# Graph network with mixture-of-experts layers: masks, scaling, weight loads and message buffers in the sum by source rearranged

## The chip, the cores and the metric

The kernel runs on one core of a Trainium2 chip. A core has five engines, each with a queue of its own that it works off in order: TensorE (PE; its weight loads are listed apart as PEld), VectorE (DVE), ScalarE (ACT), GpSimd (POOL) and SyncE (SP), which here only issues transfers. Sixteen DMA engines move data between device memory and the on-chip memory, SBUF; TensorE writes its products to PSUM, from which VectorE or ScalarE take them. The metric is the device time of one execution in microseconds, the median of several.

## The reference

Node features `x` (6250 x 256, float32) pass four residual blocks: a graph convolution with a two-layer perceptron, a top-2 mixture of 8 experts, a relational graph convolution with 8 relations, and a top-2 mixture of 6 experts. There are 100,000 edges, sorted by their `dst` and in random order of `src`. The change is in the first block and in the dispatch of its result to the experts of the second:

```python
norm = dinv[row_sl] * ew_sl * dinv[col_sl]      # row = src, col = dst, with self loops
msgs = xw[col_sl] * norm[:, None]               # one message for each edge
h7 = segment_sum(msgs, row_sl, num_segments=N) + b
h = relu(h7 @ W1 + b1); out = h @ W2 + b2
...
logits = tokens @ router_w.T                    # top-2 experts for each node
h = gelu(tokens @ w1[e] + b1[e]); y = h @ w2[e] + b2[e]
```

So each node sums the messages of the edges of which it is the source, the sum is scaled by `dinv` of that node, goes through the perceptron, and is then routed to two experts.

## The kernel before

Nodes are cut into 49 blocks of 128, which lie in SBUF as `acc` (the sums) and `X` (the features). The program runs in stages: it builds tables of the edges; it makes the messages and writes each to a place in device memory that puts the edges of one source block together (`msgs`, L858, by indirect transfers from GpSimd); it sums the messages by source and sends each finished block of nodes to the experts (`sum_and_send`, L1181); it runs the experts' tiles (L1297 to L1357); then come the relational convolution and the last experts.

The change lies in the sum stage. `sum_messages` (L874) works through 830 tiles of 128 messages in chunks of 8, so 104 chunks. For one chunk SyncE loads `g` (128 x 8 x 260 floats, 1040 KB, L880); VectorE computes `key` (L882), the place of each message's node within its block, or a value that fits none; eight one-hot masks `m` (128 x 128) are then made by comparing the row of lane numbers with the key: VectorE makes four in one instruction (L884) and GpSimd four in four instructions (L892). TensorE multiplies each mask with the tile's messages (L895) into PSUM, of which the pool `p_mm` has four buffers, and VectorE adds the product to the block's place in `acc` (L897). That place is only known at run time, so the address comes from a register, and the framework orders each such addition against every other use of `acc`.

The pool `sum` gives `g` and `key` three buffers each (`bufs=3`, L1185), and `m` two. A load of a chunk waits until TensorE has done the last tile of the chunk whose buffer it takes.

`send_group` (L1063) takes four finished blocks at a time. It is written as a generator: after each tile of the sum (L1198 to L1200) one piece of it is put in, so that its work is mixed with the sums. For each block it scales the sum by `dinv` (`h7`, L1072, on ScalarE), transposes it on TensorE, applies bias and Relu on ScalarE (L466), multiplies by `W2` (L1089), normalizes, computes the router's logits (L1110, L1119), picks two experts with some fifty small VectorE instructions, and writes each node's row to its two experts' places with eight indirect transfers from GpSimd (L1170). The group of blocks is started when a fixed number of tiles is summed (L1200).

The order of the instructions on each engine is fixed when the program is built: a scheduler of the framework takes the instructions as they are written, with its own estimates of their lengths, and places them in each engine's queue. An instruction that waits holds all that stand behind it on its engine.

Ahead of the stage, SyncE loads the first weights of the eight experts (`fw1`, eight transfers of 256 KB, L1027 through L1010) and their biases as rows (`fb1`, 1 MB written, L1028 through L1020); the second weights and biases (L1212, L1213) follow the stage. `sum_and_send` is built twice, for graphs whose blocks are done late and early (L1207 to L1210); the early one (tags with an `e`, as `pa0e`) runs here.

Of the kernel before, what the change touches and what calls it, by code (L numbers as in the profile page):

```python
# [8 lines left out]
F32 = mybir.dt.float32  # L9
# [5 lines left out]
AF = mybir.ActivationFunctionType  # L15
OP = mybir.AluOpType
# [4 lines left out]
D = 256  # L21
# [21 lines left out]
RW = 260  # L43
# [13 lines left out]
def gnn_ffn_kernel(ctx: ExitStack, tc: tile.TileContext, a, out):  # L57
    nc = tc.nc

    const = ctx.enter_context(tc.tile_pool(name="const", bufs=1))  # L60
# [5 lines left out]
    def psum_mm(name):  # L66
        return p_mm.tile([128, 512], F32, tag="mm", name=name)
# [36 lines left out]
    ones = const.tile([128, 128], F32, name="ones")  # L104
    nc.vector.memset(ones, 1.0)
    lanes_i = const.tile([128, 128], I32, name="lanes_i")
    nc.gpsimd.iota(lanes_i, pattern=[[1, 128]], base=0, channel_multiplier=0)
    lanes = const.tile([128, 128], F32, name="lanes")
    nc.vector.tensor_copy(lanes, lanes_i)
    lanes_h = const.tile([128, 128], BF16, name="lanes_h")  # L110
    nc.vector.tensor_copy(lanes_h, lanes_i)
    rev_i = const.tile([128, 1, 8], I32, name="rev_i")
# [13 lines left out]
    col0, n = {}, 0  # L126
    for name in (
# [8 lines left out]
        k = math.prod(ap.shape) // 128  # L136
# [174 lines left out]
    for q0 in range(0, QN, 4):  # L311
        n = min(4, QN - q0)
# [23 lines left out]
    far = sp.tile([128, QN], F32, name="far")  # L336
# [13 lines left out]
    turn = gap.tile([128, Q * 128], F32, name="turn")  # L350
# [52 lines left out]
    def blocks_of(blk, t0, engines, top):  # L403
        _, v = nc.values_load_multi_w_load_instructions(
            blk[0:1, t0 : t0 + 8],
            engines=engines,
            min_val=0,
            max_val=top,
            skip_runtime_bounds_check_because="it is counted or bounded",
        )  # L410
        return v

    def rsqrt(name, v, shape, pool=None):

        r = work.tile(shape, F32, name=f"{name}_r", tag="rs_r", bufs=1)
        h = work.tile(shape, F32, name=f"{name}_h", tag="rs_h", bufs=1)
        o = (pool or const).tile(shape, F32, name=f"{name}_o", tag="rs_o" if pool else f"{name}_o")
        nc.scalar.activation(h, v, AF.Sqrt)
        nc.vector.reciprocal(r, h)
        nc.vector.tensor_mul(h, r, r)  # L420
        nc.vector.tensor_mul(h, h, v)
        nc.vector.tensor_scalar(h, h, -0.5, 1.5, op0=OP.mult, op1=OP.add)
        nc.vector.tensor_mul(o, r, h)
        return o
# [32 lines left out]
    def transpose_to(name, dest, x, bias=None):  # L457

        pt = p_tr.tile([128, 2, 128], F32, tag="tr", name=f"pt_{name}")
        for k in range(2):  # L460
            nc.tensor.transpose(pt[:, k, :], x[:, k * 128 : (k + 1) * 128], ident)  # L461
        if bias is None:
            nc.scalar.copy(dest, pt)
        else:
            for k in range(2):
                nc.scalar.activation(dest[:, k, :], pt[:, k, :], AF.Relu, bias=bias[k])  # L466
# [224 lines left out]
    firsts = g0p.tile([128, TL], F32, name="firsts")  # L691
# [61 lines left out]
    dinv = rsqrt("deg", deg, [128, NT])  # L753
# [6 lines left out]
    acc = big.tile([128, (NT + 1) * D], F32, tag="big", name="acc0")  # L760
# [113 lines left out]
    def sum_messages(pool, tag):  # L874

        for t0 in range(0, TL, 8):
            n = min(8, T - t0)
            blocks = blocks_of(blks, t0, [ENG.DVE], NT)
            g = pool.tile([128, 8, RW], F32, name=f"g0{tag}_{t0}", tag="g")
            nc.sync.dma_start(g, by_tile[:, t0 : t0 + 8, :])  # L880
            key = pool.tile([128, 8], F32, name=f"key{tag}{t0}", tag="key")
            nc.vector.tensor_sub(key[:, :n], g[:, :n, D], firsts[:, t0 : t0 + n])  # L882
            m = pool.tile([128, 8, 128], F32, name=f"m0{tag}_{t0}", tag="m", bufs=2)
            nc.vector.tensor_tensor(  # L884
                m[:, :4],
                lanes[:, None, :].to_broadcast([128, 4, 128]),
                key[:, :4, None].to_broadcast([128, 4, 128]),
                OP.is_equal,
            )
            for j in range(n):  # L890
                if j >= 4:
                    nc.gpsimd.tensor_scalar(m[:, j], lanes, key[:, j : j + 1], None, op0=OP.is_equal)  # L892
            for j in range(n):
                ps = psum_mm(f"pa0{tag}_{t0 + j}")
                nc.tensor.matmul(ps[:, :D], m[:, j, :], g[:, j, :D], start=True, stop=True)  # L895
                here = acc[:, bass.ds(blocks[j] * D, D)]
                nc.vector.tensor_add(here, here, ps[:, :D])  # L897
                yield t0 + j + 1
# [107 lines left out]
    def load_experts(pool, name):  # L1006
        n_e = a[name].shape[0]
        w = pool.tile([128, n_e, 2, D], F32, name=f"w_{name}")
        for e in range(n_e):
            nc.sync.dma_start(w[:, e], a[name][e].rearrange("(k p) f -> p k f", p=128))  # L1010
        return w


    def rows_of(name, pool):

        v = a[name]
        k = math.prod(v.shape)
        r = pool.tile([128, k], F32, name=f"rows_{name}")
        flat = v.rearrange("(o n) -> o n", o=1) if len(v.shape) == 1 else v.rearrange("e (o n) -> o (e n)", o=1)
        nc.sync.dma_start(r, flat.to_broadcast([128, k]))  # L1020
        return r
# [2 lines left out]
    ys = dram.tile([TE * 128, D], F32, name="ys")  # L1024
    ffn0 = ctx.enter_context(ExitStack())
    fp = ffn0.enter_context(tc.tile_pool(name="ffn0", bufs=1, side="right"))
    fw1 = load_experts(fp, "L0_ffn_w1").rearrange("p e k f -> p (e k f)")  # L1027
    fb1 = rows_of("L0_ffn_b1", fp)  # L1028
    share1 = const.tile([128, NT], F32, name="share1")
    share2 = const.tile([128, NT], F32, name="share2")  # L1030
    ats = const.tile([128, 2, NT], I32, name="ats")
# [31 lines left out]
    def send_group(g, n, mlp, tag, seen):  # L1063
# [5 lines left out]
        for i in range(n + 1):  # L1069
            if i < n:  # L1070
                h7 = work.tile([128, D], F32, name=f"h7{tag}_{g + i}", tag="xn", bufs=3)
                nc.scalar.activation(  # L1072
                    h7, acc[:, (g + i) * D : (g + i + 1) * D], AF.Copy, scale=dinv[:, g + i : g + i + 1]
                )
                rows.append(h7)
            if i:
                transpose_to(
                    f"h7{tag}_{g + i - 1}",
                    uT[:, :, (i - 1) * 128 : i * 128],
                    rows[i - 1],  # L1080
                    [b_mlp[:, k : k + 1] for k in range(2)],
                )
            yield
# [97 lines left out]
    def sum_and_send(tag, early):  # L1181


        with (
            tc.tile_pool(name=f"sum{tag}", bufs=3, side="right") as sump,  # L1185
            tc.tile_pool(name=f"mlp{tag}", bufs=1) as mlp,
        ):
            seen, steps, waiting = [], None, list(GROUPS)

            def step(through):  # L1190
                nonlocal steps
                if steps is None and waiting and through(sum(waiting[0])):
                    g, n = waiting.pop(0)
                    steps = send_group(g, n, mlp, tag, seen)
                if steps is not None and next(steps, steps) is steps:
                    steps = None

            for turn in sum_messages(sump, tag):  # L1198
                if early:
                    step(lambda blocks: S_TURNS * blocks + S_SLACK <= turn)  # L1200
            while steps is not None or waiting:
                step(lambda blocks: True)
# [4 lines left out]
    with tc.If(nlate_sv > 0) as late_s_cmp:  # L1207
        sum_and_send("l", False)
    with late_s_cmp.Else():
        sum_and_send("e", True)  # L1210
    fp2 = ffn0.enter_context(tc.tile_pool(name="ffn0b", bufs=1, side="right"))
    fw2 = load_experts(fp2, "L0_ffn_w2").rearrange("p e k f -> p (e k f)")  # L1212
    fb2 = rows_of("L0_ffn_b2", fp2)  # L1213

    def in_stages(stages, items):

        held = [None] * len(stages)
        for i in range(len(items) + len(stages) - 1):
            for k in reversed(range(len(stages))):
                if 0 <= i - k < len(items):  # L1220
                    held[k] = stages[k](*(held[k - 1] if k else items[i]))
# [144 lines left out]
    acc = big.tile([128, (NT + 1) * D], F32, tag="big", name="acc1")  # L1366
# [285 lines left out]
```

## Time and profile before

| | |
|---|---|
| median of 3 runs | 4226.73 us (4225.7 to 4229.28) |
| profiled execution | 4228.4 us, its span 4226.6 us |
| mean granted TensorE clock | 0.92 of full speed |
| busy over the span | PE 3488.2 us, DVE 2093.3, ACT 1194.2, POOL 2266.0 |
| messages made and written (391 to about 1427 us) | GpSimd busy with 782 indirect transfers |
| sum by source and sends (1440 to 2184 us) | 830 tiles, 49 scalings, 98 sends |
| experts' tiles (2209 to 2480 us) | 105 tiles |
| table of the second convolution (2480 to 2955 us) | |
| second convolution and last experts (2955 us to the end) | |

The span is counted from the first instruction to the last. In the profile an instruction is named by its line, its engine, and the tiles it writes and reads (`acc<-acc,pa0e`); an `x` and a number give how many such instructions are in the row. In a timeline, the bracket behind a row is the time that the engine stood idle before it and what ended that wait. Where several waits end together, the profile names the one that came last. SPq is SyncE's queue.

### The profile page before, as it was taken

Reading aid. Unit: us, or ns where it says so; the run is one execution under the profiler, and the core shown is the slowest. Engines: PE = TensorE matmul, PEld = TensorE weight load, DVE = VectorE, ACT = ScalarE, POOL = GpSimd, SP = SyncE. Lnnn points to the kernel's source line nnn. Section 1 sums busy time; section 2 is a strip of 40 time slices with the busy share of each in tenths; the row PEclk is TensorE's granted clock in tenths of the full one; section 3 lists DMA queues with packets and bytes.
Section 4 is the critical chain, followed back from the end, with each engine's and each line's share of the span. In section 5 each row is a group of like instructions: output and inputs, shape, how many; then the busy total and the mean of one; then the engine's idle time right before and its main releaser. Section 6 shows DMA issues by size and latency. Waiting matters only on the chain.

```text
span 4226.6 us, 52427 instructions
## 1 busy us (share of the span) xinstructions
PE 3488.2 (83%) x14645; PEld 2318.7 (55%) x14645; DVE 2093.3 (50%) x5670; ACT 1194.2 (28%) x2567; POOL 2266.0 (54%) x2440
## 2 busy tenths in 40 slices
PE   2887777777777467888869977999579999999999
PEld 1565665565656344555547743444256666666656
DVE  6686211111111146777763358665456666666552
ACT  3312333333333101111114433665012222222213
POOL 1001777777777524555551048333767777777650
PEclk7998999999999778999989988999689999999999
DMA  5514333333333424555543335444645555555540
GB/s 176 168 37 154 129 128 128 128 128 128 127 128 129 148 97 166 182 183 191 182 160 124 109 104 201 196 196 204 191 142 151 150 153 152 150 150 153 143 116 9
DMA packets 233062, 612.03 MB, mean 145 GB/s; under 512 B 41909, under 2 KB 126104, under 8 KB 212784
## 3 DMA queue, kind: packets, MB, share of 16 engines
q0 software_dynamic: 100624, 294.88, 22.3%
q1 hardware_dynamic: 112636, 290.21, 20.4%
q10 hardware_dynamic: 19488, 23.31, 1.5%
q8 instruction: 131, 2.15, 0.2%
q14 instruction: 183, 1.49, 0.1%
HBM read 371.49 MB, written 236.79 MB: 144 GB/s over the span
## 4 chain that ended last, share of the span: by engine, by line
PE 38%; DVE 9%; issue 4%; DMA 2%; ACT 2%; POOL 2%; DVEq 0%; ACTq 0%; POOLq 0%; SPq 0%
PE ph_e1a L473 6%; PE py1a L1001 5%; PE pa1a L922 5%; PE ph_e2a L473 5%; PE phx L1415 4%; PE pf L1334 2%; PE pf L1350 2%; PE pa0e L895 2%; DVE rest L1425 1%; DVE acc L897 1%; DVE acc L926 1%; PE pt_fh L461 1%; DMA g1a<-hx,idxT 1%; DVE hx L1409 1%; PE pcb1a L1517 1%
## 5 line engine op out<-in xcount | busy, mean ns | idle before, releaser
L858 POOL DMA_INDIRECT msgs<-msgn,at x782 | 785.9, 1005 | 550.7 <-DMA rowsn<-lane_rows 312.9
L914 POOL DMA_INDIRECT g1a<-hx,idxT x830 | 828.3, 998 | 323.2 <-PE pa1a L922 144.9
L840 PE MATMUL pxn<-acc,sTn 128*128 x3128 | 790.8, 413 | 243.1 <-DVE sTn L821 216.2
L840 PEld LDWEIGHTS pxn<-acc,sTn 128*128 128x128 f32 x3128 | 613.5, 206 | 420.3 <-DVE sTn L821 282.4
L895 PE MATMUL pa0e<-g0e,m0e 128*128 128x256 f32 x1660 | 502.1, 440 | 186.2 <-DVE acc L897 79.2
L855 ACT ACTIVATE msgn<-pxn,ewT 128x256 f32<-128x256 f32 x782 | 370.0, 473 | 638.4 <-PE pxn L840 451.0
L926 DVE TENSOR_TENSOR acc<-acc,pa1a 128x256 f32 x830 | 346.9, 418 | 343.2 <-PE pa1a L922 312.4
L895 PEld LDWEIGHTS pa0e<-g0e,m0e 128*128 128x128 f32 x1660 | 298.2, 209 | 355.9 <-DVE acc L897 136.2
L892 POOL TENSOR_SCALAR m0e<-lanes,keye 128x128 f32<-128x128 f32 x414 | 265.9, 657 | 346.9 <-PE pa0e L895 274.7
L831 DVE COPY msgn<-srcT 128x32 f32<-128x32 f32 x98 | 18.0, 186 | 830.2 <-DMA msgs<-msgn,at 748.1
L922 PE MATMUL pa1a<-g1a,m1a 128*128 128x256 bf16 x2490 | 374.8, 282 | 54.4 <-DMA g1a<-hx,idxT 38.6
L897 DVE TENSOR_TENSOR acc<-acc,pa0e 128x256 f32 x830 | 347.4, 419 | 126.9 <-ACT h7e L1072 41.6
L922 PEld LDWEIGHTS <-m1a 128*128 128x128 bf16 x2490 | 243.4, 100 | 278.3 <-issue 193.7
L1415 PE MATMUL phx<-wr,xT 128*128 128x512 f32 x784 | 373.5, 621 | 24.9 <-DVE rest L1425 19.1
L1001 PE MATMUL py1a<-w_L_ffn_expert_w,v2a 128*128 128x256 f32 x1176 | 285.8, 383 | 6.4 <-DVE acc L926 3.4
L473 PE MATMUL ph_e1a<-xT3a,w_L_ffn_expert_w 128*128 128x512 f32 (+2 forms) x672 | 288.9, 556 | 0.0
L473 PE MATMUL ph_e2a<-v1a,w_L_ffn_expert_w 128*128 128x512 f32 (+2 forms) x672 | 280.6, 543 | 2.1 <-DVE acc L926 1.3
L480 ACT ACTIVATE v1a<-ph_e1a,cols 128x512 f32<-128x512 f32 (+2 forms) x168 | 106.5, 634 | 539.7 <-PE ph_e1a L473 539.5
L1415 PEld LDWEIGHTS phx<-wr,xT 128*128 128x128 f32 x784 | 150.1, 199 | 186.3 <-issue 164.4
L1375 POOL DMA_INDIRECT y<-ys,ats x98 | 97.4, 994 | 278.4 <-issue 263.6
L1001 PEld LDWEIGHTS py1a<-w_L_ffn_expert_w,v2a 128*128 128x128 f32 x1176 | 208.6, 190 | 44.4 <-ACT v2a L480 10.2
L1002 DVE SCALAR_TENSOR_TENSOR X<-py1a,C1a,X 128x256 f32<-128x256 f32 x294 | 139.0, 481 | 112.3 <-PE py1a L1001 111.3
(643 smaller groups left out, 4261.8 us busy)
## 6 DMA issues: line engine op xcount, KB each, us to landing
g0e<-msgs SPq DMA_DIRECT2D x104, 1040.0 KB
hx<-hx SPq DMA_DIRECT2D x49, 1536.0 KB
rowsn<-lane_rows SPq DMA_DIRECT2D x98, 256.0 KB
fx<-xs SPq DMA_DIRECT2D x105, 128.0 KB
ys<-fy ACTq DMA_DIRECT2D x105, 128.0 KB
g1a<-hx,idxT POOLq DMA_INDIRECT x830, 3.1
msgs<-msgn,at POOLq DMA_INDIRECT x782, 2.6
msgs<-none ACTq DMA_DIRECT2D x10, 650.0 KB
```

The costliest lines, as they stand in the source:

```text
L473: nc.tensor.matmul(ps[:, :ncols], w[:, k, f * 128 : (f + 1) * 128], xT[:, k, :ncols], start=(k == 0), stop=(k == 1),)
L840: nc.tensor.matmul(come, sT[:, k, j, :], acc[:, bass.ds(blocks[j] * D + k * D, D)], start=(k == 0), stop=(k == 1),)
L855: nc.scalar.activation(msg[:, j, :D], come, AF.Copy, scale=ewT[:, t0 + j : t0 + j + 1])
L858: ins = nc.gpsimd.indirect_dma_start(out=msgs, out_offset=bass.IndirectOffsetOnAxis(ap=at[:, t0 + j : t0 + j + 1], axis=0), in_=msg[:, j, ...
L892: nc.gpsimd.tensor_scalar(m[:, j], lanes, key[:, j : j + 1], None, op0=OP.is_equal)
L895: nc.tensor.matmul(ps[:, :D], m[:, j, :], g[:, j, :D], start=True, stop=True)
L897: nc.vector.tensor_add(here, here, ps[:, :D])
L914: nc.gpsimd.indirect_dma_start(out=g, out_offset=None, in_=table, in_offset=bass.IndirectOffsetOnAxis(ap=idxT[:, t0 + j : t0 + j + 1], axi ...
L922: nc.tensor.matmul(ps[:, :D], m[:, j, :], g[:, k * D : (k + 1) * D], start=(k == 0), stop=(k == 2))
L926: nc.vector.tensor_add(here, here, ps[:, :D])
L1001: nc.tensor.matmul(ps[:, :D], hT[:, k, j : j + 128], w[:, k, :], start=(k == 0), stop=(k == 1))
L1415: nc.tensor.matmul(ps, xT[:, k, :], wr[:, k, r : r + 2, :].rearrange("p r o -> p (r o)"), start=(k == 0), stop=(k == 1),)
```

## The change

Five things are done. `g` gets four buffers instead of three. Of a chunk's eight masks VectorE makes two instead of four, in one instruction of half the size; two are made on ScalarE, each by two instructions: the absolute value of lane number plus (negated) key, and then Relu of one minus that, which is one where the key fits and zero elsewhere; GpSimd makes the same four as before. For this the key is negated, and a tile `minus` of negated lane numbers is made once at the start, with which VectorE and GpSimd compare. The scaling `h7` is done by VectorE instead of ScalarE. The eight loads of `fw1` are no longer issued ahead of the stage but written into its loop, one with each of the chunks 5 to 12. The load of `fb1` is written behind the stage, between the second weights and their biases.

```diff
@@ constants
+    minus = const.tile([128, 128], F32, name="minus")
+    nc.vector.tensor_scalar(minus, lanes_i, -1.0, None, op0=OP.mult)
@@ sum_messages
-            g = pool.tile([128, 8, RW], F32, name=f"g0{tag}_{t0}", tag="g")
+            g = pool.tile([128, 8, RW], F32, name=f"g0{tag}_{t0}", tag="g", bufs=4)
...
-            nc.vector.tensor_sub(key[:, :n], g[:, :n, D], firsts[:, t0 : t0 + n])
+            nc.vector.tensor_sub(key[:, :n], firsts[:, t0 : t0 + n], g[:, :n, D])
             m = pool.tile([128, 8, 128], F32, name=f"m0{tag}_{t0}", tag="m", bufs=2)
             nc.vector.tensor_tensor(
-                m[:, :4],
-                lanes[:, None, :].to_broadcast([128, 4, 128]),
-                key[:, :4, None].to_broadcast([128, 4, 128]),
+                m[:, :2],
+                minus[:, None, :].to_broadcast([128, 2, 128]),
+                key[:, :2, None].to_broadcast([128, 2, 128]),
                 OP.is_equal,
             )
-            for j in range(n):
-                if j >= 4:
-                    nc.gpsimd.tensor_scalar(m[:, j], lanes, key[:, j : j + 1], None, op0=OP.is_equal)
+            for j in range(2, n):
+                if j < 4:
+                    far = pool.tile([128, 128], F32, name=f"far{tag}{t0}_{j}", tag="far", bufs=2)
+                    nc.scalar.activation(far, lanes, AF.Abs, bias=key[:, j : j + 1])
+                    nc.scalar.activation(m[:, j], far, AF.Relu, bias=ones[:, 0:1], scale=-1.0)
+                else:
+                    nc.gpsimd.tensor_scalar(m[:, j], minus, key[:, j : j + 1], None, op0=OP.is_equal)
@@ ahead of the stage
-    fw1 = load_experts(fp, "L0_ffn_w1").rearrange("p e k f -> p (e k f)")
-    fb1 = rows_of("L0_ffn_b1", fp)
+    fw1 = fp.tile([128, 8, 2, D], F32, name="fw1")
@@ send_group
-                nc.scalar.activation(
-                    h7, acc[:, (g + i) * D : (g + i + 1) * D], AF.Copy, scale=dinv[:, g + i : g + i + 1]
+                nc.vector.tensor_scalar(
+                    h7, acc[:, (g + i) * D : (g + i + 1) * D], dinv[:, g + i : g + i + 1], None, op0=OP.mult
                 )
@@ sum_and_send
             for turn in sum_messages(sump, tag):
+                if turn % 8 == 0 and 5 <= turn // 8 < 13:
+                    e = turn // 8 - 5
+                    nc.sync.dma_start(fw1[:, e], a["L0_ffn_w1"][e].rearrange("(k p) f -> p k f", p=128))
@@ behind the stage
     fw2 = load_experts(fp2, "L0_ffn_w2").rearrange("p e k f -> p (e k f)")
+    fb1 = rows_of("L0_ffn_b1", fp2)
     fb2 = rows_of("L0_ffn_b2", fp2)
+    fw1 = fw1.rearrange("p e k f -> p (e k f)")
```

## The prediction

> **What bounds the kernel now.** I read first the busy time by stage. All edits act between the last message sent (1427 us) and the first expert tile (2209 us), so this stage is split where its pace changes (columns: stretch, length, then busy time and count of TensorE, weight load, VectorE, ScalarE, GpSimd; granted clock; DMA share; GB/s).
>
> ```profile
> 1440.00:1645.00 205.00, 135.00 (x397) 89.79 (x398) 93.04 (x283) 13.58 (x34) 66.34 (x93) 0.75 0.35 120
> 1645.00:2184.00 539.00, 450.21 (x1866) 296.82 (x1866) 406.41 (x1481) 82.28 (x222) 287.48 (x410) 0.96 0.55 184
> ```
>
> The first 21 chunks of 8 tiles take 205 us (9.8 each) with every engine partly idle; the other 83 take 539 (6.5 each), with VectorE and TensorE both full. ScalarE has room in both. The timeline of one early chunk shows why the first stretch is slow:
>
> ```profile
> 1483.09 20.88 SPq L880 DMA_DIRECT2D g0e<-msgs  x3
> 1483.09 0.69 DVE L884 TENSOR_TENSOR m0e<-lanes,keye 128x512 f32<-128x512 f32 x1 [1.83 <-PE pa0e L895]
> ...
> 1488.01 0.17 DVE L882 TENSOR_TENSOR keye<-g0e,firsts 128x8 f32<-128x8 f32 x1 [3.44 <-DMA g0e<-msgs]
> 1488.16 0.42 DVE L897 TENSOR_TENSOR acc<-acc,pa0e 128x256 f32 x1
> 1488.64 5.22 PE L895 MATMUL pa0e<-g0e,m0e 128*128 128x256 f32 x12 [3.32 <-DVE acc L897]
> ```
>
> A load goes out when TensorE leaves a chunk's last tile (1483.1) and lands 4.9 us later. VectorE's key of that chunk stands in its queue ahead of sums that are ready, so it holds them for 3.4 us; PSUM fills and TensorE stops too, then does six tiles in 5.2 us at a low clock. Load 4.9 + six tiles 5.2 + key = the 10.3 us that chunks 3 to 11 take. I call this the locked cycle. Then the waits of the whole stage (total, times, longest) and the groups:
>
> ```profile
> POOL m0e L892 <- PE pa0e L895: 274.7, 61, 14.1
> DVE keye L882 <- DMA g0e<-msgs: 78.8, 27, 16.2
> DVE acc L897 <- ACT h7e L1072: 41.6, 43, 4.2
> PE pa0e L895 <- POOL m0e L892: 37.4, 12, 6.0
> ```
>
> ```profile
> L897 DVE TENSOR_TENSOR acc<-acc,pa0e 128x256 f32 x830 | 347.4, 419 | 126.9 <-ACT h7e L1072 41.6 <-PE pa0e L895 41.1 <-DVE acc L897 6.4
> L884 DVE TENSOR_TENSOR m0e<-lanes,keye 128x512 f32<-128x512 f32 x104 | 73.1, 703 | 26.9 <-PE pa0e L895 25.7 <-PE prke L1148 1.0
> L466 ACT ACTIVATE uTe<-pt_h7e,b_mlp 128x128 f32<-128x128 f32 x98 | 33.5, 363 | 43.2 <-PE pt_h7e L461 43.2
> L1072 ACT ACTIVATE h7e<-acc,deg_o 128x256 f32<-128x256 f32 x49 | 24.6, 502 | 445.3 <-DVE acc L897 445.3
> ```
>
> Of the 78.8 us of key waits 69.8 fall before 1650. In the later stretch VectorE paces: its sums follow each other every 0.525 us (0.42 busy, the rest register work). Two places stand out there, in the timeline of one group:
>
> ```profile
> 1993.84 0.97 POOL L1170 DMA_INDIRECT xs<-toke,ats  x1 [0.30 <-issue]
> 1994.85 7.17 POOL L892 TENSOR_SCALAR m0e<-lanes,keye 128x128 f32<-128x128 f32 x12
> 1995.53 3.47 PEld L895 LDWEIGHTS pa0e<-g0e,m0e 128*128 128x128 f32 x10 [3.69 <-POOL m0e L892]
> ...
> 2000.45 0.42 DVE L897 TENSOR_TENSOR acc<-acc,pa0e 128x256 f32 x1 [0.64 <-ACT h7e L1072]
> 2001.21 0.50 ACT L1072 ACTIVATE h7e<-acc,deg_o 128x256 f32<-128x256 f32 x1
> 2001.75 0.42 DVE L897 TENSOR_TENSOR acc<-acc,pa0e 128x256 f32 x1 [0.87 <-ACT h7e L1072]
> ```
>
> GpSimd's eight sends (10.2 us) hold its masks back, and TensorE stops 3.7 us. Then, where a group's sums are scaled, sum and ScalarE scaling alternate at 1.3 us a tile.
>
> **The Trainium skill.** "DMA: Bandwidth & Descriptors" (its fit of about 2.0 us plus bytes over 436e3 per us) gives 4.4 us for 1040 KB: the trace has 4.9, so most of a load is transfer and a fourth buffer shortens nothing by itself. "TensorE: Matmul & The Clock Gate", Part 1, says that idle windows halve the array clock: the trace agrees (0.75 granted in the slow stretch, 0.96 after). "ScalarE: Activation LUTs", What ACT_TABLE_LOAD costs, prices an ACTIVATE with a pointer bias at 280 ns + 0.833 per element, 387 ns for 128, with 93 ns overlap back to back; L466 is the nearest row, 363. Table sets says that abs and relu are in every set, so no table is loaded more; no run here shows it yet.
>
> **The change part by part.** Where instructions land is read from the built program's issue order on each engine; only the sum stage and its loads differ.
>
> *Fourth message buffer.* In the old order, the key of chunk 4 stands behind sum 14, of chunk 5 behind sum 22, and so on: one tile before the tile that frees its buffer. In the new order the key of chunk 5 stands behind sum 14, of chunk 6 behind sum 22. The keys have moved one chunk ahead, so each still stands one tile before its buffer's release, and the locked cycle stays. Counting keys at such a place: 15 before, 14 after (the last, behind sum 134, becomes one seven tiles late enough). One locked chunk less: 10.3 − 6.5 = −4 us. A gain from the buffer beyond this is bounded by the 14 stalls left: 0 to −60 (rival 1). In the later stretch the distance from release to key averages about seven tiles in both. Keys keep three buffers, so a key also waits for GpSimd's masks three chunks back; those stand before the tiles in question: 0, at most +1 us a group after the sends.
>
> *Weights.* Eight loads and the bias rows leave SP's queue ahead of the sums: 1427.97 to 1432.59, so the first message load comes 4.6 us sooner. But in the issue order all eight new loads follow the fourth message load in one run, not one per chunk. Four message loads at 2.5 us each (keys at 1445.1, 1447.6, 1450.1) end near 1448, the 2 MB of weights at the 300 GB/s seen at 1430 to 1438 take 6.5 to 7 more, then the fifth chunk lands near 1457; the old fourth, at the same sum, landed at 1457.0. Gain at the head: 0 (−4 to +2). The bias rows (1 MB, some 2.7 us at 370 GB/s) go behind the second weights at 2183; those transfers end by 2191, first use is at 2214, covered: 0, and 2.7 if that cover were gone.
>
> *Masks.* VectorE makes 2 of 8: 256 elements at the 0.42 of a 128x256 tensor op against 0.70, −0.28 x 104 = −29 us of VectorE. It is worth time only where VectorE paces: not in the 21 slow chunks; not in the two chunks a group that run into GpSimd's sends (21 chunks), where a sooner arrival just waits; and about 20 more lie under the group's own matmuls, where TensorE paces. 41 chunks x 0.28 = −11 (bounds 0 and −29). ScalarE gains four instructions a chunk, 416 x 0.3 to 0.39 = 125 to 160 us, of some 650 idle. They precede their tile by 8 or more tiles, and cost only by standing ahead of a group's L466 and copies: two chunks a group, 0 to 2.9 us; I take 0.3, +3. GpSimd's four masks and sends do not change.
>
> *Scaling on VectorE.* 49 scalings of 128x256 leave ScalarE (0.50) for VectorE; L1479, a tensor-scalar op of that size, takes 0.41 (bounds 0.27 to 0.5). The alternation becomes 0.525 + 0.47 = 1.0 us a tile against 1.3, then TensorE (tile 0.43, transposes 0.44, two-part product 0.86) paces: −0.3 x 42 tiles after 1645 = −13, and −1 for the earlier ones. A transposed tile waits for VectorE instead of ScalarE, no longer than before. One constant at the start (0.4 us) lies beside loads.
>
> Sum: −4 + 0 − 11 + 3 − 14 = −26. The profiled execution took 4228.4 (span 4226.6), 1.7 over the median 4226.73; from the median, 4201 us.
>
> **Rivals.** (1) The fourth buffer does free the early chunks. For it: 69.8 us of key waits. Against: the issue order, key by key. 14 chunks x (10.3 − 6) = −60, so about 4140 with the rest. (2) What VectorE saves is given back at GpSimd's sends and the group matmuls. For it: 274.7 us of GpSimd waiting for TensorE shows that masks depend on released buffers, not speed. Then only the early −4 and a few us stay: 4218 to 4228. (3) Slower: ScalarE, in order, becomes the wait. A Relu mask waits for TensorE to leave the chunk two back, and L466 of a group waits behind it. Price: eight instructions (2.9 us) and about 2 us of release wait per group, x 12 = +59, less 27: near 4259. It decides once a group loses over 2.2 us so. Against: L466 has slack now (no TensorE wait on it is listed), and the masks stand between transposes that come later anyhow. (4) VectorE paces more than I allow, or the ends of the bounds add: −29 − 21 − 8, about 4170 (4166 to 4182).
>
> **How the numbers follow.** Forecast (4182 to 4217) 0.60; rival 1 0.08; rival 2 0.14; rival 3 0.08; rival 4 0.10. The range 4166 to 4228 holds all but rivals 1 and 3. Within 0.2% (8.5 us) is what a measurement here can hardly tell from no change: of rival 2, 0.11. Faster 0.60 + 0.08 + 0.10 + 0.03 = 0.81, slower 0.08.
>
> **What would show it.** Right: chunks 4 to 11 still 10 to 10.5 us apart with keys waiting 3 us for loads; the stretch before 1645 shorter by 5 us at most; eight weight loads in one run; no VectorE wait on a scaling; L884 near 0.42; later chunks about 6.2 us. Wrong: early chunks near 6 us (rival 1); TensorE or the L466 group waiting for ScalarE masks (rival 3); longer TensorE waits on GpSimd with the later stretch unchanged (rival 2).

## The result, and the profile after

The changed kernel takes 4183.9 us (median, 4183.09 to 4185.12) where the kernel before takes 4226.39 beside it: a ratio of 0.9899, 95% interval 0.9884 to 0.9914, so 42.5 us less (36 to 49). The forecast was 26 less, 4201 us; the result lies in its range, near the low end. The profiled execution took 4184.4 us, its span 4182.6.

First the busy time by stage (columns as in the prediction; the second stretch ends with the last sum, at 2142 us now):

```profile
1440.00:1645.00 205.00, 137.76 (x419) 91.18 (x417) 95.61 (x313) 40.18 (x119) 64.00 (x97) 0.79 0.38 131
1645.00:2142.00 497.00, 436.16 (x1828) 287.96 (x1826) 392.18 (x1493) 168.85 (x498) 280.03 (x403) 0.96 0.57 193
```

The early stretch is what it was: as slow, the clock as low, only ScalarE has work in it now. It ends 8 us sooner in the order of the chunks (chunk 20's masks are 8.4 us earlier). The last sum comes 41 us sooner, so the later stretch gave the other 33 (539 and 497 us are both counted from 1645 and have the 8 us in them). An early chunk, in the timeline:

```profile
1500.55 10.68 SPq L882 DMA_DIRECT2D g0e<-msgs  x2
...
1500.63 0.42 DVE L886 TENSOR_TENSOR m0e<-minus,keye 128x256 f32<-128x256 f32 x1 [1.72 <-PE pa0e L901]
...
1505.68 0.17 DVE L884 TENSOR_TENSOR keye<-firsts,g0e 128x8 f32<-128x8 f32 x1 [3.84 <-DMA g0e<-msgs]
1505.84 0.42 DVE L903 TENSOR_TENSOR acc<-acc,pa0e 128x256 f32 x1
1506.38 0.30 PEld L901 LDWEIGHTS pa0e<-g0e,m0e 128*128 128x128 f32 x2 [4.13 <-issue]
...
1510.98 0.43 DVE L886 TENSOR_TENSOR m0e<-minus,keye 128x256 f32<-128x256 f32 x1 [1.69 <-PE pa0e L901]
```

This is the locked cycle of the prediction, with a fourth buffer: a load at 1500.55, the key that waits 3.84 us for it in front of sums that are ready, TensorE idle for 4 us. VectorE's masks of the next chunk follow 10.3 us after the first ones shown, as before. The waits of the whole stage (total, times, longest) and the groups:

```profile
ACT m0e L896 <- PE pa0e L901: 332.5, 88, 10.7
POOL m0e L898 <- PE pa0e L901: 275.7, 67, 14.5
...
DVE keye L884 <- DMA g0e<-msgs: 76.3, 24, 8.5
...
PEld pa0e L901 <- ACT m0e L896: 23.2, 44, 0.8
...
PE pa0e L901 <- POOL m0e L898: 22.9, 12, 4.4
```

```profile
L903 DVE TENSOR_TENSOR acc<-acc,pa0e 128x256 f32 x830 | 347.2, 418 | 92.7 <-PE pa0e L901 42.9 <-DVE acc L903 6.5 <-DVE placee L1161 2.0
...
L896 ACT ACTIVATE m0e<-fare,ones 128x128 f32<-128x128 f32 x208 | 73.2, 394 | 351.3 <-PE pa0e L901 332.5 <-PE prke L1153 18.6
L895 ACT ACTIVATE fare<-lanes,keye 128x128 f32<-128x128 f32 x208 | 72.7, 392 | 96.2 <-DVE keye L884 69.4 <-DVE seene L1143 24.5 <-DVE acc L903 2.2
...
L886 DVE TENSOR_TENSOR m0e<-minus,keye 128x256 f32<-128x256 f32 x104 | 44.3, 426 | 37.4 <-PE pa0e L901 36.0 <-PE prke L1153 1.1
...
L1077 DVE TENSOR_SCALAR h7e<-acc,deg_o 128x256 f32<-128x256 f32 x49 | 20.9, 428 | 2.4 <-PE pt_h7e L463 0.4
```

The prices were right: the halved mask takes 426 ns (forecast 0.42 us), the scaling 428 in the mean (0.41), each half of a ScalarE mask 392 to 394, beside 387, an estimate from the formula in the Trainium skill ("ScalarE: Activation LUTs", What ACT_TABLE_LOAD costs). ScalarE loads a table five times in each of the two traces, once in this stage, so the new functions added no load. The 41.6 us in which sums waited for ScalarE's scaling are gone, and waits for ScalarE's masks are short (0.8 us at most). What the forecast does not have is the drop of TensorE's waits for GpSimd's masks, 37.4 to 22.9 us. It stands in three places. The lead of the changed kernel is measured here at VectorE's masks, and averaged over four to six chunks, as single ones scatter by 2 to 4 us. It grows by 5 us around chunk 50 (14.8 to 19.8 us), by 9 around chunk 84 (24.1 to 32.9) and by 7 around chunk 92 (32.9 to 39.8); from chunk 21 to 48 it grows by 7 in all. At these three places, and only there, a group's eight sends come at another place of GpSimd's queue: behind the masks of chunks 50, 83 and 91, where they stood ahead of them.

### The profile page after: what moved, and what is told of

Read it like the earlier page. It is cut to its first block, busy times and chain, and to the rows that moved or that the text cites. A ratio compares the mean times of both kernels' runs of the same rounds, so it can differ in the third digit from the quotient of the medians.

```text
span 4182.6 us, 53223 instructions
## 1 busy us (share of the span) xinstructions
PE 3478.2 (83%) x14645; PEld 2313.5 (55%) x14645; DVE 2083.1 (50%) x5720; ACT 1310.2 (31%) x2934; POOL 2261.2 (54%) x2440
## 4 chain that ended last, share of the span: by engine, by line
PE 41%; DVE 12%; DMA 5%; issue 5%; POOL 2%; ACT 2%; DVEq 1%; ACTq 0%; SPq 0%; POOLq 0%
PE ph_e1a L475 6%; PE py1a L1007 6%; PE pa1a L928 6%; PE ph_e2a L475 5%; PE pa0e L901 4%; PE phx L1425 4%; DMA g0e<-msgs 3%; DVE acc L903 3%; PE pf L1344 2%; PE pf L1360 2%; DVE rest L1435 1%; DVE acc L932 1%; PE pt_fh L463 1%; DVE hx L1419 1%; PE pg2e L1094 1%
## 5 line engine op out<-in xcount | busy, mean ns | idle before, releaser
L898 POOL TENSOR_SCALAR m0e<-minus,keye 128x128 f32<-128x128 f32 x414 | 259.5, 641 | 320.0 <-PE pa0e L901 275.7
L1007 PEld LDWEIGHTS py1a<-w_L_ffn_expert_w,v2a 128*128 128x128 f32 x1176 | 208.8, 190 | 44.2 <-ACT v2a L482 10.3
```

The lines of the kernel that those rows point to most:

```text
L898: nc.gpsimd.tensor_scalar(m[:, j], minus, key[:, j : j + 1], None, op0=OP.is_equal)
L1007: nc.tensor.matmul(ps[:, :D], hT[:, k, j : j + 128], w[:, k, :], start=(k == 0), stop=(k == 1))
```

## The experiments

All stage times below are from the first to the last of VectorE's 104 mask instructions in the trace: 725.8 us before, 694.5 after. Each is from one execution. Four runs (keys later on the kernel before, old masks, weights in later chunks, third mask) were on two other chips, on which the kernel before takes some 4540 us: the stage begins about 135 us later there, and what follows it takes some 180 us longer. The stage itself keeps its pace: the run with weights in later chunks and the one that it changes are of two chips, and from chunk 6 to the end the second stays 4.1 to 5.0 us behind. So for these four read ratios and stage times, not medians.

**The sends' place alone, added and taken back.** In both kernels only the order of GpSimd's queue differs, by edges that set the order within that queue and add no wait:

```diff
@@ send_group, on the kernel before: groups 5, 9, 10 behind the masks of chunks 50, 83, 91
+                tc.add_manual_dep(ins.ins, masks_of[tag, chunk].ins.name, NoSync)
@@ sum_messages, on the changed kernel: those masks behind the sends
+                    tc.add_manual_dep(cmp.ins, send.ins.name, NoSync)
```

> The kernel before, with one thing moved: three of GpSimd's eleven groups of eight sends (those of groups 5, 9 and 10) stand in its queue behind the four masks of chunks 50, 83 and 91 instead of ahead of them, which is where the changed kernel has them. No other instruction of any engine changes its place. Theory A (the sends' place gave about half of the gain: in the trace after, chunks 48 to 52, 81 to 86 and 89 to 93 each gain 7 to 9 us, and nothing else stands there): 18 to 24 us faster, about 4206 us, and TensorE's wait at these three places falls from 5 to 6 us to 1 to 2. Theory B (VectorE's relief by masks and scaling gave all of the later stretch): within 4 us of the kernel before, 4226.

> The changed kernel, with the same three groups of sends put back ahead of the masks of chunks 50, 83 and 91; nothing else moves. Theory A: 18 to 24 us of the 42.5 are lost, so 4202 to 4208 us, 0.994 to 0.996 of the kernel before. Theory B: no loss, 4184 us within 4.

Measured: the sends moved, 4212.96 us, ratio 0.9975 (0.9967 to 0.9983): 10.6 us less (7 to 14), stage 713.5. Put back in the changed kernel, 4198.34 us, ratio 0.9937 (0.9923 to 0.9950) against 0.9899: 16 us lost (8 to 24, from the two intervals); stage 711.6, so 17 more. The traces put the difference at the three places: with the sends moved alone, the lead over the kernel before grows by 2.4, 5.2 and 2.5 us there and by 1 in all the rest of chunks 20 to 100; with them put back, the changed kernel loses 6 to 8 us at each. TensorE's longest wait for GpSimd's masks at these groups is 5.2, 6.4 and 5.5 us before, 3.0, 2.0 and 4.4 with the sends moved, 1.8, 1.3 and 2.2 in the changed kernel, and 6.8, 6.4 and 7.3 with the sends put back. So the place does matter, and it is not the whole late gain: on its own half of what I expected, in the changed kernel a little less than that. The traces say why it differs. A mask can only be made when TensorE has left the chunk two back, so masks are at most two chunks ahead of the sums. When GpSimd began these three groups' sends, it had made masks for 8, 8 and 7 tiles beyond the last sum begun (counted in the trace before), for 14 each in the trace after, for 12, 12 and 10 with the sends moved alone, and for only 6, 8 and 5 with them put back. A tile takes 0.525 us at the pace of the sums, the sends 10.2: 8 tiles cover 4.2 us, 14 cover 7.4. Here is one such group in GpSimd's timeline, with the weight load of TensorE that waits for it, first with the sends put back:

```profile
2016.50 1.05 POOL L1185 DMA_INDIRECT xs<-toke,ats  x1 [4.64 <-DVE ats L1181]
...
2027.59 4.68 POOL L901 TENSOR_SCALAR m0e<-minus,keye 128x128 f32<-128x128 f32 x8
...
2028.29 5.13 PEld L911 LDWEIGHTS pa0e<-g0e,m0e 128*128 128x128 f32 x14 [6.43 <-POOL m0e L901]
```

and in the changed kernel:

```profile
2011.56 2.38 POOL L898 TENSOR_SCALAR m0e<-minus,keye 128x128 f32<-128x128 f32 x4 [3.25 <-PE pa0e L901]
2014.11 1.06 POOL L1175 DMA_INDIRECT xs<-toke,ats  x1 [0.16 <-DVE m0e L886]
...
2024.34 4.80 POOL L898 TENSOR_SCALAR m0e<-minus,keye 128x128 f32<-128x128 f32 x8
...
2025.03 0.30 PEld L901 LDWEIGHTS pa0e<-g0e,m0e 128*128 128x128 f32 x2 [1.29 <-POOL m0e L898]
```

Ahead of the masks, GpSimd waits 4.64 us for the sends' addresses, in the last 1.5 of which it could have begun the masks of that chunk (ScalarE's begin at 2015.03), and then sends for 11 us. Behind them, it makes these masks first, and the first send then waits only 0.16 us. TensorE's wait falls from 6.43 to 1.29 us; in the kernel before, at the same group, it is:

```profile
2048.95 4.92 PEld L895 LDWEIGHTS pa0e<-g0e,m0e 128*128 128x128 f32 x14 [6.36 <-POOL m0e L892]
```

The faster VectorE gets to that point, the sooner the sums catch up with the masks in hand, and the more a wrong place costs.

**Scaling alone, masks alone.** The edits are those of the change; for the masks one ordering edge keeps the tenth group's sends where the kernel before has them.

> The kernel before with only the scaling of the sums (49 of 128x256) moved from ScalarE to VectorE. GpSimd's and SyncE's queues are the same; VectorE's keys too, but for chunk 19, which stands eight tiles later (one stall for a load fewer). The prediction's step: -14 for the scaling and -4 for the stall, about 4209 us. Theory A, in which masks and scaling together are worth about -11: -5 to -8 and -4, about 4215. If the scaling is off the path: 4223 to 4227.

> The kernel before with only the masks split (VectorE makes two of eight, ScalarE two with two instructions each, the key negated), and the sends kept where they stand in the kernel before; scaling on ScalarE, three message buffers, weights ahead of the stage. The prediction's step: -11 + 3 = -8, about 4219 us. Theory A: -3 to -6, 4221 to 4224. If ScalarE's masks hold up its copies of the groups, which here still include the scalings: 4227 to 4240.

Measured: scaling 4203.18 us, 0.9947 (0.9934 to 0.9961), 22 us less (16 to 28); stage 712.9. Masks 4216.04 us, 0.9981 (0.9972 to 0.9989), 8 us less (5 to 12); stage 716.5. By the medians theory A, with 11 for both, falls: they gave what the prediction said (18 with the stall, and 8) or somewhat more. The stage is less clear on the scaling: it is 13 us shorter, in an execution (4211.1 us) that is the slowest of its five. From the first to the fourth scaling of a group, with three sums between them, it took 6.0 us in the mean of twelve groups before (3.9 to 7.5), 5.0 with the scaling alone and 4.9 after. The stall is seen too: between chunks 16 and 25 of the run with the scaling alone, where the key of chunk 19 stands later, 5.6 us of lead come and stay.

**Fourth buffer undone, weights alone.**

```diff
@@ on the changed kernel, GpSimd's queue held as it is
-            g = pool.tile([128, 8, RW], F32, name=f"g0{tag}_{t0}", tag="g", bufs=4)
+            g = pool.tile([128, 8, RW], F32, name=f"g0{tag}_{t0}", tag="g")
```

> The changed kernel with three message buffers; GpSimd's queue, with all its sends, is held as the changed kernel has it. With three buffers the keys stand one chunk nearer again, one tile ahead of the tile that frees their buffer: chunks 3 to 12, 14, 15, 17 and 18, so 14 stalls, as many as the changed kernel has (chunks 4 to 13, 15, 16, 18 and 19). Theory A (the fourth buffer only moves the keys and, through the order, two of the sends): 4184 within 4. If the buffer's extra distance is used in the later stretch: 4190 to 4200. If the change were right that it frees the early chunks, more than 4220.

> The kernel before with only the loads of the first weights moved into the loop and the bias rows behind the stage. VectorE's, ScalarE's and GpSimd's queues are the same. The prediction's step: 0 (-4 to +2), since the eight loads follow the message loads in one run. The trace after has the first chunk 7.7 us sooner, of which 2.9 are left by chunk 4: so 0 to 4 us faster, 4220 to 4224; more than 6 faster would mean that it is the weights that help elsewhere too.

Measured: three buffers 4185.48 us, 0.9919 (0.9905 to 0.9932) against the changed kernel's 0.9899: 8 us more by the ratios, but 0 to 17 by their intervals, and the stage has 693.0 us against 694.5. So the early chunks owe the buffer nothing, and whether it is worth some us as such is not decided. In the traces three buffers are 4 us ahead by chunk 8 and lose as much again after chunk 50. There GpSimd begins the three groups' sends with masks for 10, 10 and 13 tiles in hand, instead of 14, and over the stage TensorE's weight loads wait 90.0 us for GpSimd's masks instead of 69.0. Weights alone 4213.33 us, 0.9984 (0.9977 to 0.9990): 6.8 us less (4 to 10), more than either bound of the prediction. With three buffers the eight weight loads follow the third message load and cost one message load 1.5 us (6.45 where it took 4.9). In the run with the weights alone the first message load goes out 8.0 us sooner than before, counted from the first issue behind the message stage, so the head alone accounts for some 6.5. With four they follow the fourth, and the trace after has lost 4.8 us of its 7.7 by chunk 4. The fourth buffer's own effect at the head is thus a small loss. Built with three buffers and no edges, the changed kernel has only the tenth group's sends behind the next masks: that group was moved by the masks, and the other two move only with the fourth buffer.

**The locked cycle.** The key is held behind a sum, by an ordering edge within VectorE's queue:

```diff
@@ on the changed kernel (17), and on the kernel before (9; there the sends are held where they were)
+            sub = nc.vector.tensor_sub(key ...)
+            tc.add_manual_dep(sub.ins, sum_of[tag, t0 - 17].ins.name, NoSync)
```

> The changed kernel, with the key of each chunk c held in VectorE's queue behind the sum of tile 8c - 17 (eight tiles after the tile whose end frees the buffer of its load) where it stands in front of it now (behind sum 8c - 26, one tile ahead of that tile, for chunks 5 to 12 and five more). No other order changes but a few masks and matmuls around the keys; the sends stay where the changed kernel has them. The prediction's locked cycle (the key, ahead of sums that are ready, makes load and sums follow one another): chunks 4 to 11 stand 6 to 7 us apart where they stand 10.3, 14 such chunks x 3.3 to 4 us = 45 to 55 us less, 4130 to 4140 us. If the early chunks are slow for another cause (the transfers themselves, the low clock, GpSimd): less than 15 us, 4170 to 4184.

> The kernel before, three message buffers and all, with the key of each chunk c held behind the sum of tile 8c - 9, eight tiles after the tile that frees the buffer of its load (8c - 17); GpSimd's queue, with all its sends, is the same as before, TensorE's and ScalarE's nearly. If the stall comes from the key's place alone, as the locked cycle has it, no fourth buffer is needed: chunks 4 to 11 about 5.1 us apart as in the run with keys eight tiles later, some 15 stalls x 5.2 = 60 to 80 us less, 4140 to 4160 us. If the fourth buffer is needed for it (the masks, made so late, come late themselves): less than 30 us, 4190 or more.

Measured: on the changed kernel 4103.19 us, 0.9722 (0.9709 to 0.9736), so 1.8% or 75 us (66 to 83) beyond the change; stage 612.0, of which 74 us are gained by chunk 20. Chunks 4 to 11 stand 5.1 us apart where they stood 10.3. The same 80 us of the two traces, by busy time, of the changed kernel and then with the keys later:

```profile
1465.00:1545.00 80.00, 46.88 (x128) 30.84 (x128) 30.37 (x79) 10.85 (x34) 20.63 (x32) 0.83 0.31 103
```

```profile
1465.00:1545.00 80.00, 68.51 (x258) 41.57 (x257) 58.18 (x197) 25.19 (x70) 40.60 (x60) 0.94 0.53 186
```

Twice the matmuls of all kinds, at a clock of 0.94 instead of 0.83. The waits of keys for loads in the run with the keys later:

```profile
DVE keye L886 <- DMA g0e<-msgs: 14.0, 4, 8.5
```

They were 76.3 us in 24. On the kernel before, with three buffers, the ratio is 0.9883 (0.9863 to 0.9902), 53 us less (45 to 62); the stage 667.6 us, 58 less, a little under the forecast. Chunks 4 to 11 are 5.4 us apart. So the place of the key makes the stall, and no fourth buffer is needed to end it; but GpSimd's masks now wait for their key in the second stretch, as the waits before and then in this run show:

```profile
POOL m0e L892 <- DVE keye L882: 40.5, 9, 9.6
...
POOL m0e L905 <- DVE keye L887: 103.0, 22, 9.7
```

From chunk 20 on a chunk takes 6.57 us instead of 6.37, which gives 17 us back. With four buffers there is room for the key both 8 tiles behind the release and 17 ahead of its chunk. That the fourth buffer is good for this is read from the two runs together; it was not tried apart.

**Both cures together, and what each part is worth then.**

```diff
@@ sends: two blocks behind the masks of one chunk, two behind the next; keys behind sum 8c - 17
+            behind = chunk_of_group[g] + i // 2
```

> The changed kernel with both: keys behind sum 8c - 17 as in the run with keys eight tiles later, and each group's eight sends split into four behind the masks of one chunk and four behind those of the next. Theory A (a group of eight sends, some 10 us of GpSimd, is longer than what the two mask buffers cover, and its place matters for that reason): beyond the keys 10 to 25 us more, since the eleven groups still cost TensorE 2.5 to 5.7 us each in the trace after: 4105 to 4125. If the sends no longer cost: the same as with the keys alone. If they delay the sends of the last groups into the experts' part: slower than with the keys alone.

> The run with keys eight tiles later and split sends, with the masks shared as before: VectorE four of eight, ScalarE none. The sends and keys stay in place. Masks alone gave 8 us on the kernel before, of 29 that VectorE saves (0.28 x 104). If the other 21 had been given back at stalls for loads and sends (the prediction's reason for counting only 41 of the 104 chunks), they show up here, where these stalls are gone: 20 to 29 us slower than 4074, 4094 to 4103. If TensorE paces where VectorE does not, masks are worth no more here: 4078 to 4086.

Measured: 4074.0 us (4069.59 to 4077.02), 0.9651 (0.9638 to 0.9664), stage 583.7: 29 us beyond the keys alone, a little more than expected, and 3.5% below the kernel before. From the first to the fourth scaling it takes 3.2 us in the mean here, at most 3.9: what was longer before went with the sends. With the masks shared as before in this kernel, the ratio is 0.9737 (0.9712 to 0.9762), the stage 615.5: 32 us more, a little over the forecast, and 36 by the ratios (24 to 48). The same edit gave 8 us on the kernel before. VectorE saves 29 us either way; with the stalls for loads and sends in place most of it is given back.

**Weights in later chunks, and a third mask on ScalarE.**

```diff
@@ loads of fw1 behind the message load of chunk 40 and later
-                if turn % 8 == 0 and 5 <= turn // 8 < 13:
+                if turn % 8 == 0 and 40 <= turn // 8 < 48:
+                    tc.add_manual_dep(ins.ins, load_of[tag].ins.name, NoSync)
@@ and, for the second run
-                if j < 4:
+                if j < 5:
```

> The run with keys eight tiles later and split sends, with the eight weight loads held in SyncE's queue behind the message load of chunk 40 or a later one each, where they now follow the fourth message load in one run. Nothing else moves. The prediction's step: the 2 MB of weights stand between the fourth and the fifth message load and delay them; without them the step from chunk 3 to chunk 4 (9.6 us in that run) falls to 5 to 6: 3 to 5 us faster than 4074. If the four message loads at the head set that step, no change.

> The run with weights in later chunks (keys eight tiles later, split sends), with one more of GpSimd's masks made on ScalarE, so VectorE two, ScalarE three, GpSimd three. TensorE's, VectorE's and SyncE's orders stay but for one key. In that run the weight loads still wait 54.9 us for GpSimd's masks (73 times) and 17.1 for ScalarE's. If GpSimd's masks are what is left to gain: that wait falls below 25 us and the 104 chunks take 10 to 25 us less than the 578.6 us there (0.62 us less on GpSimd a chunk). If ScalarE becomes the wait instead (the prediction's third rival: 0.79 us more a chunk on an engine that also has to serve the groups): waits for ScalarE's masks over 50 us, and 0 to 20 us more than 578.6.

Measured: weights later, ratio 0.9669 (0.9645 to 0.9694), stage 578.6: the step from chunk 3 to 4 falls from 9.6 to 5.1 us, and the stage by 5.1, about as expected; ratios of two chips can't show so little. The third mask on ScalarE: ratio 0.9672 (0.9650 to 0.9693), stage 583.4, 5 us more. The waits of the two runs, first with two masks on ScalarE:

```profile
PEld pa0e L916 <- POOL m0e L913: 54.9, 73, 1.4
...
PEld pa0e L916 <- ACT fare L910: 19.1, 8, 17.1
...
PEld pa0e L916 <- ACT m0e L911: 17.1, 35, 0.8
```

then with three:

```profile
PEld pa0e L916 <- ACT fare L910: 65.1, 77, 15.0
...
PEld pa0e L916 <- ACT m0e L911: 13.1, 45, 0.8
```

(The profile puts some waits for ScalarE down to `far`, the first half of a mask; the longest, 17.1 and 15.0 us, are the start of the stage.) Waits for GpSimd's masks fall from 54.9 to 1.5 us, and waits for ScalarE take their place: 63 us without the start, where they were 19. So the third rival's mechanism exists, with three masks of eight on ScalarE, not with two. That it makes the stage longer is not shown: of the 5 us, from two executions on two chips, half come by chunk 21.

## Why the prediction was right, and where its sum was wrong

The sign, the order of size and the slow early stretch were foreseen; 16 of 42.5 us were not. That the result still fell into the range, 2 us from its end, is in part luck: a term of 11 to 16 us was missing. Of the signs named, one failed: the early stretch became 8 us shorter, where 5 was the most allowed. Later chunks take 6.0 us, where about 6.2 was forecast. By the steps:

- *The locked cycle stays.* Right, read from the issue order alone: the trace after shows it line by line, and moving the keys alone ends it. This also settles rival 1: the fourth buffer frees nothing while the keys move ahead with it.
- *Fourth buffer, −4, one stall fewer.* The count of 14 stalls is right, but the step credited the wrong edit. With three buffers the changed kernel has 14 as well, because the scaling on VectorE moves the key of chunk 19. What the buffer itself is worth is not resolved (0 to 17 us by the ratios, nothing by the stage); a little is lost at the head, and two groups of sends move with it, which the step did not have. The price of a stall was too low: 10.3 − 6.5 = 3.8 us was taken with the pace of the later stretch; with no group's work mixed in, a chunk takes 5.1, so 5.2 a stall, 73 for 14, and the keys' run gained 74 by chunk 20.
- *Weights, 0 at the head.* The eight loads in one run, and the loss to them by chunk 4, were right. The gain of the first chunk was 7.7 us instead of 4.6, and 2.9 were left: inside the bounds given (−4 to +2). Alone, with three buffers, the step is worth 6.8, outside them: the term for what the loads cost was worked out for four buffers.
- *Masks, −11 and +3.* Measured alone, −8. Right, and for the reason given: of the 29 us that VectorE saves, most meets a stall.
- *Scaling, −14.* Measured alone −22 (16 to 28) with the stall of chunk 19 in it, for which the prediction's terms give 18. The trace shows 13 in the stage. Right in mechanism; the size is not resolved more closely than that.
- *"GpSimd's four masks and sends do not change."* This is the step that failed. Their number and kind did not change; the place of three groups of sends in the queue did. The prediction takes the keys' and loads' places one by one, and the sends' as given. The term is −11 on the kernel before and −16 in the changed one. With the second the sum −26 becomes −42, but that closeness has errors of some us in it: the parts measured alone (scaling, masks, weights, sends) add to 48, each with an interval of 3 to 6 us either way.
- *Rival 2*, savings given back at the sends, holds in part: for masks, 21 of 29 us. *Rival 4* has a time near the result (4166 to 4182), for another reason. *Rival 3* did not come true with two masks on ScalarE.

My first theory after the result, that masks and scaling gave only 11 and the sends 20, had the sends about twice too large for the kernel before, where they gave 10.6. The lead in the trace at three places mixes both: what VectorE saves between groups is lost or kept there.

## What to carry to other kernels

When an order is fixed at build time, a large part of an edit's effect, here 11 to 16 of 42 us, can lie in instructions that it does not touch: compare the place of every blocking instruction, on every queue, before pricing the edit. For a transfer or send that stands in a compute queue, count the work in hand when it starts, here 8 or 14 tiles, against its length. A waiting instruction is cured by its place: a key held 8 tiles later in its queue was worth 75 us, where another buffer, with the key moved ahead along with it, ended none of the stalls.

## What the runs showed that was not expected

- The slow early stretch costs twice: with the keys moved, the clock of the same 80 us rises from 0.83 to 0.94, and a matmul of the sum takes 434 ns in the mean there instead of 521. "TensorE: Matmul & The Clock Gate", Part 1, in the Trainium skill has idle windows halve the array clock; here ending the idle time raised the granted mean.
- A group of eight sends holds GpSimd some 10.2 us: about 0.97 us busy for each and 0.30 between two. Split into four and four, with the keys later, the same sends cost 29 us less over eleven groups.
- The first message load went out 7.5 us sooner, where the emptier queue was to give 4.6. The branch into the stage came 5.5 us sooner (1434.84 to 1429.33 us), and the gap from it to the load shrank from 5.3 to 3.3 us (2.6 in the two runs with moved weights and three buffers). Why it shrank was not tested.
